# Selective-scan layer on one core: three small VectorE/GpSimd operations change engines, and one fetch moves up by a unit

## The chip, the cores and the metric

One core of a Trainium2 chip runs the whole program, four layers in one launch. The metric is the device time of one execution in microseconds, the median of several runs. VectorE is called DVE here, ScalarE ACT, GpSimd POOL, TensorE PE, and SP is the engine whose queue issues nearly all DMAs.

## The reference, cut to what matters

The input is eight images of 64 channels by 64 x 64. Layer 0 is a selective-scan block; layers 1 to 3 are attention and a small trained modifier, and the change doesn't touch them. In layer 0, after a norm, an input projection to a scanned half and a gate half z, and a depthwise convolution, four scans run over each image's 4096 places: along rows, along columns, and both backwards. Each has 128 channels and 16 states n:

```
h = h * exp(dt * A[n]) + dt * B[n] * u          # per place, channel and n
y = sum over n of h * C[n]                      # then summed over the four scans
y = layernorm(y) * silu(z);  out = x + y @ outproj
```

B and C come from projections of u and are the same for all 128 channels. silu(z) * layernorm(y) is the gating product that the change is about. dt is a softplus.

## The kernel before, in words

The scan layer is `scan_layer`. A *step* is one scan direction k and one chunk of 1024 places; an image has 16 steps, in the order k = 0, 2, 1, 3 (1, 3, 0, 2 for the last image), four chunks each. A step has 16 *units*, one for each state n; the code counts units as turns. The order of instructions on each engine is written out by hand, in the loop from L888 on.

In unit n of a step:

- SP loads C's row n, broadcast to 128 partitions, into a `ct` tile one unit ahead (L715; five `ct` buffers), and for the units 0, 3, 6 and 8 (`BY_POOL`, L704) B's row likewise into `bt`.
- ACT makes a = exp(dt * A[n]) two units ahead (L719).
- B * dt * u goes to a PSUM tile z in one of two ways. In `BY_POOL` units POOL multiplies `bt` by dt*u (L727) and ACT copies it to PSUM (L734). In the other twelve PE spreads B's row over the partitions (L737), and DVE multiplies that in place by dt*u (L764).
- DVE runs the scan h (L768), reading a from SBUF and z from PSUM. POOL multiplies h by C's row (L773), and PE adds the product into y's sum (L810, three units later), which frees the `ct` buffer.

For the spreading by PE, B is split into three bf16 pieces whose sum is B. This is done once for each chunk and each k of 0 and 1, so eight times an image, by `pieces`: fetch B (L673, SP), first piece (L677, ACT), subtract (L681, POOL), second piece (L684, ACT), third piece (L687, a subtraction on POOL), three stores (L692, SP), and a load in the spread form (L699, SP). These functions are called from `hooks`: a hook of unit n is called behind everything else of unit n. For a step with all seven pieces they stand at units 7 to 13. The softplus of the next step (`soft1`, `soft2` on ACT, `soft3` on POOL, L645) stands at 6, 7 and 8, and dt*u (L664, POOL) at 11.

Work of the neighbouring images (the norm, the convolution, the gate, the output projection) is a queue of small items (`Background`), at most one for each unit, and none at units 3, 6, 7 and 8 but for those without a PE part. The output part of the previous image, `norm_y` and `after`, is queued at unit 4 of step 0. Its `apply` puts y * rstd on DVE (L450) and gain and bias on ACT (L451), and behind these calls `multiply` (L564 to L566) for the block before: z *= y, 128 x 512, on POOL. PE projects the product out later (L573). z was fetched from DRAM three blocks ahead (L561).

Of the kernel before, what the change touches and what calls it, by code (L numbers as in the profile page):

```python
# [13 lines left out]
ALU = mybir.AluOpType  # L14
# [8 lines left out]
BK = 512  # L23
# [211 lines left out]
def scan_layer(cm, x_in, w, xh):  # L235

    tc, nc = cm.tc, cm.nc
    with ExitStack() as ctx:
# [63 lines left out]
        for e in range(2):  # L302
            r = slice(e * C, (e + 1) * C)
# [20 lines left out]
        def bank(name):  # L324
            return psum.tile([128, BK], F32, name=name, tag="mm")
# [226 lines left out]
        def after(b, y, zd, blocks=range(NBK)):  # L552

            xf = x_in[b].rearrange("c h w -> c (h w)")
            gated = {}

            def load(j):
                xr = work.tile([C, BK], F32, name="xr", tag="xr", bufs=3)
                nc.sync.dma_start(xr, xf[:, bass.ts(j, BK)])
                z = work.tile([DI, BK], F32, name="z", tag="z", bufs=3)  # L560
                nc.sync.dma_start(z, zd[:, bass.ts(j, BK)])  # L561
                gated[j] = (xr, z)

            def multiply(j):  # L564
                z = gated[j][1]
                nc.gpsimd.tensor_tensor(z, z, y[:, bass.ts(j, BK)], ALU.mult)  # L566

            def project_out(j):
                def make():
                    po = bank("ops")  # L570
                    xr, z = gated[j]
                    nc.tensor.matmul(po[:C], cm.ident[:C, :C], xr, start=True, stop=False)
                    nc.tensor.matmul(po[:C], wout, z, start=False, stop=True)  # L573
                    return po

                def use(po):
                    del gated[j]
                    xo = work.tile([128, BK], F32, name="xo", tag="sq")
                    nc.scalar.activation(xo[:C], po[:C], AF.Identity, bias=outb)
                    bg.later(lambda: nc.sync.dma_start(xh[b][:, bass.ts(j, BK)], xo[:C]))  # L580
                    if j + 3 in blocks:
                        load(j + 3)

                return make, use

            return norm_y(y, blocks, load, multiply, project_out)

        def ordered(t, k, c):
# [73 lines left out]
        def step_input(ctl):  # L662

            nc.gpsimd.tensor_tensor(ctl["dus"], ctl["dt"], ctl["ut"]["u"], ALU.mult)  # L664


        def pieces(ctl, low):

            by_place = "a n (j x) -> (n j) a x"

            def fetch():
                low["b"] = work.tile([128, 2, 128], F32, name="bw", tag="bw", bufs=1)
                nc.sync.dma_start(low["b"], low["bc"][:, :N].rearrange(by_place, x=128))  # L673

            def first():
                low["p"] = work.tile([128, 3, 2, 128], BF16, name="bp", tag="bp", bufs=1)
                nc.scalar.copy(low["p"][:, 0], low["b"])  # L677

            def subtract():
                low["r"] = work.tile([128, 2, 128], F32, name="br", tag="br", bufs=1)  # L680
                nc.gpsimd.tensor_tensor(low["r"], low["b"], low["p"][:, 0], ALU.subtract)  # L681

            def second():
                nc.scalar.copy(low["p"][:, 1], low["r"])  # L684

            def third():
                nc.gpsimd.tensor_tensor(low["p"][:, 2], low["r"], low["p"][:, 1], ALU.subtract)  # L687

            def store():
                low["bsd"] = dr.tile([2, 3 * N, CH], BF16, name="bsd", tag="bsd", bufs=8)  # L690
                for i in range(3):
                    nc.sync.dma_start(  # L692
                        low["bsd"][:, i * N : (i + 1) * N].rearrange(by_place, x=128),
                        low["p"][:, i],
                    )

            def get():
                ctl["bs"] = work.tile([3 * N, CH], BF16, name="bs", tag="bs")
                nc.sync.dma_start(ctl["bs"], low["bsd"][ctl["k"] // 2])  # L699

            return ([fetch, first, subtract, second, third, store] if ctl["k"] < 2 else []) + [get]


# [75 lines left out]
        def empty():  # L779

            if full:
                ctl = full.pop()
                nc.scalar.copy(
                    ordered(ctl["y"], ctl["k"], ctl["c"]),
                    ctl["ps"].rearrange("p (a b) -> p a b", b=S),
                )
# [85 lines left out]
        with tc.manual_schedule():  # L872
# [15 lines left out]
            for b in range(NB):  # L888
                for s in range(4 * NCH):


                    early, late = b == 0 and s + 1 < NCH, b == NB - 1 and s > 3 * NCH
                    if s + 1 < 4 * NCH:
                        nxt = prepare(b, s + 1)
                    else:
                        nxt = prepare(b + 1, 0)
                    bg.credit = 2 if b == NB - 2 else 1
                    idle = () if early or late else (3, 6, 7, 8)
                    hooks = {}
                    if nxt:  # L900
                        do = nxt["pieces"]
                        if early:
                            hooks = {
                                12: [do[0]], 13: [nxt["soft"][2], lambda: step_input(nxt)] + do[1:5],
                                14: do[5:6], 15: do[6:],
                            }
                        else:
                            hooks = {14 - len(do) + i: [f] for i, f in enumerate(do)}
                            for i, f in zip((6, 7, 8), nxt["soft"]):
                                hooks[i] = hooks.get(i, []) + [f]  # L910
                            hooks[11] = hooks.get(11, []) + [lambda: step_input(nxt)]

                    def ahead(do, m, *args):
                        if m < N:
                            do(ctl, m, *args)
                        elif nxt:
                            do(nxt, m - N, *args)

                    for n in range(N):
                        empty()  # L920
                        ahead(spread, n + 1)
                        slots = 0 if early or late else sum(m not in idle for m in range(n, N))
                        if n == LAG + 1:
                            bg.before(n in idle, slots)
                            begin_sum()
                        else:
                            if len(pending) > LAG:
                                sum_up()
                            if n == LAG + 5:
                                sum_up()  # L930
                            bg.before(n in idle, slots)
                        if (n + 5) % N in BY_POOL and not (early and n + 5 == N):
                            ahead(load, n + 5, 0)
                        ahead(load, n + 1, 1)
                        ahead(decay, n + 2)
                        save_state()
                        if n + 3 != N or not early:
                            ahead(product, n + 3)
                        unit(ctl, n)
                        bg.after()  # L940
                        for _ in range(bg.surplus(max(0, 11 - n)) if early else late):
                            bg.before()
                            bg.after()
                        for do in hooks.get(n, []):
                            do()
                        if n + 3 == N and early:
                            ahead(load, N, 0)
                            ahead(product, N)

                        if s == 0 and n == LAG + 2 and b > 0:  # L950
                            bg.add(after(b - 1, images[b - 1][2], images.pop(b - 1)[1]))
                        if late and n == LAG + 2:
                            c = 4 * NCH - s
                            bg.add(after(b, images[b][2], images[b][1], range(2 * c, 2 * c + 2)))
                        if s == (1 if b else NCH) and n == 0 and b + 1 < NB:
                            bg.add(later.pop(NCH, []))
                            start(b + 1)
                    if nxt:
                        if not nxt["first"]:
                            nxt["state"] = ctl["new"]  # L960
                    ctl = nxt
# [1154 lines left out]
```

## Time and profile before

| what | us |
|---|---|
| median of 3 runs | 12470.36 (12468.33 to 12488.72) |
| the profiled execution, its own time | 12474.25 |
| its span on the core | 12472.4 |
| scan layer within it | about 0 to 7200 |
| from 1000 to 6000: POOL busy in each 1000 | 957 to 965 |
| DVE | 937 to 948 |
| PE | 926 to 938 |
| ACT | 698 to 720 |
| DMA engines, mean share busy | 63 to 64% |

The rest of the page has three kinds of views. The shares and slices give each engine's busy time over the whole span and over 40 equal slices, as digits in tenths. The groups put together all instructions of one line, engine, operation and shape: count, then busy time in us and mean length of one in ns, then the idle time of the engine just before them and what ended it. The windows give the busy time of every engine in a chosen stretch, with the number of instructions, the granted PE clock as a share of full speed, the DMA share and the GB/s. The waits of 1000 to 7000 us are used too: SP waits 4277 us for PE's sums (L810) to free `ct` buffers, ACT waits 616 us for DVE's scans and 212 us for POOL's subtraction (L681), PE waits 326 us for DVE's scans, POOL waits 150 us for the load of `ct`, and DVE waits 144 us for PE's spread B.

### The profile page before, as it was taken

How to read it: one execution, taken by the hardware profiler on the slowest of the kernel's cores; microseconds unless marked ns; L12 is line 12 of the kernel's file. 1: busy time of each engine (PE TensorE's matmuls, PEld its weight loads, DVE VectorE, ACT ScalarE, POOL GpSimd, SP SyncE). 2: the span in 40 equal slices, each digit the busy share in tenths (PEclk: the TensorE clock that was granted, in tenths of full speed). 3: DMA queues.
4: the chain of work that ended last, by engine and by line, in shares of the span. 5: the costliest groups of instructions: out<-in, count | busy, mean ns of one | idle time of the engine just before them, and what ended most of it. 6: DMA issues, size and time to landing. Idle time of an engine off the chain costs nothing. (4 is left out here: it accounts for less than half of the span.)

```text
span 12472.4 us, 119759 instructions
## 1 busy us (share of the span) xinstructions
PE 11350.5 (91%) x38827; PEld 4100.1 (33%) x38827; DVE 10374.0 (83%) x7334; ACT 7820.0 (63%) x10296; POOL 7404.9 (59%) x3510
## 2 busy tenths in 40 slices
PE   7899998999999999999998889999987778999999
PEld 2233332332333323323322232332334463333333
DVE  4999999999999999999989857768687785676767
ACT  4776766766766767767666545546456584555554
POOL 4999999999999999999999800000005490000000
PEclk8999999999999999999989889999998789999999
DMA  3666656656666666666566510000011100000000
GB/s 110 208 210 211 210 200 221 211 202 214 210 203 212 207 212 213 202 218 205 198 206 204 179 34 18 12 25 6 18 38 40 41 24 23 17 6 17 6 11 6
DMA packets 541331, 1562.17 MB, mean 125 GB/s; under 512 B 127360, under 2 KB 144400, under 8 KB 538128
## 3 DMA queue, kind: packets, MB, share of 16 engines
q1 hardware_dynamic: 540688, 1554.36, 37.8%
q8 instruction: 310, 5.08, 0.2%
q14 instruction: 333, 2.73, 0.1%
HBM read 1456.41 MB, written 88.87 MB: 124 GB/s over the span
## 5 line engine op out<-in xcount | busy, mean ns | idle before, releaser
L773 POOL TENSOR_TENSOR ct<-ct,h 128x1024 f32<-128x1024 f32 x2048 | 4796.5, 2363 | 391.5 <-DMA ct<-bc 183.9
L768 DVE TENSOR_TENSOR_SCAN h<-a,state,z 128x1024 f32<-128x1024 f32 x1536 | 3572.4, 2342 | 96.0 <-ACT z L734 43.0
L1117 DVE TENSOR_TENSOR sum<-sum,ex 128x1024 f32<-128x1024 f32 x1920 | 2347.5, 1223 | 617.9 <-ACT ex L1110 483.0
L1110 ACT ACTIVATE ex<-sc 128x1024 f32<-128x1024 f32 x2048 | 1968.0, 1024 | 1359.7 <-PE sc L1105 1359.3
L810 PE MATMUL yps<-ct,ident 128*128 128x512 f32 x5632 | 2810.5, 629 | 6.9 <-POOL ct L773 6.8
L719 ACT ACTIVATE a<-dt,amat 128x1024 f32<-128x1024 f32 x2048 | 2345.0, 1146 | 718.1 <-DVE h L768 711.7
L764 DVE TENSOR_TENSOR z<-z,e 128x1024 f32<-128x1024 f32 x1536 | 1865.9, 1215 | 310.9 <-PE z L737 196.0
L1124 PE MATMUL av<-ex,v 128*64 128x512 f32 x8192 | 1950.0, 604 | 0.0
L1105 PE MATMUL sc<-q,k 16*128 16x512 f32 (+1 forms) x8192 | 1562.2, 623 | 4.2 <-ACT q L1098 3.1
L810 PEld LDWEIGHTS yps<-ct,ident 128*128 128x128 f32 x5632 | 1009.0, 194 | 1390.9 <-issue 1253.2
L737 PE MATMUL z<-bs,pick 48*128 48x512 bf16 x3072 | 957.0, 393 | 447.0 <-DVE h L768 398.5
L810 PE MATMUL yps<-ct,lno_cen 128*128 128x512 f32 x2560 | 1313.1, 646 | 0.5 <-POOL ct L773 0.5
L768 DVE TENSOR_TENSOR_SCAN h<-a,z 128x1024 f32<-128x1024 f32 x512 | 1163.1, 2283 | 80.8 <-ACT z L734 51.2
L727 POOL TENSOR_TENSOR bt<-bt,e 128x1024 f32<-128x1024 f32 x512 | 1210.8, 2365 | 4.5 <-DMA bt<-bc 4.5
L1431 POOL TENSOR_TENSOR gt<-gt,pad 128x1024 f32<-128x1024 f32 x16 | 34.9, 2184 | 1571.1 <-ACT gt L1430 1492.5
L1124 PEld LDWEIGHTS av<-ex,v 128*64 128x64 f32 x8192 | 512.2, 136 | 1332.8 <-issue 1278.9
L734 ACT COPY z<-bt 128x1024 f32<-128x1024 f32 x512 | 519.7, 1015 | 589.0 <-POOL bt L727 316.4
L1105 PEld LDWEIGHTS sc<-q,k 16*128 16x128 f32 (+1 forms) x8192 | 528.4, 184 | 1016.1 <-issue 977.2
L737 PEld LDWEIGHTS <-pick 48*128 48x128 bf16 x3072 | 177.7, 95 | 1709.6 <-DVE h L768 888.0
L810 PEld LDWEIGHTS yps<-ct,lno_cen 128*128 128x128 f32 x2560 | 468.6, 198 | 637.3 <-issue 560.7
L530 PE MATMUL vps<-pad,convd 128*128 128x512 f32 x1152 | 545.9, 597 | 0.0
L1804 DVE RECIPROCAL r<-e 128x512 f32<-128x512 f32 x128 | 420.6, 3322 | 0.0
(416 smaller groups left out, 10539.4 us busy)
## 6 DMA issues: line engine op xcount, KB each, us to landing
ct<-bc SPq DMA_DIRECT2D x2048, 512.0 KB
bt<-bc SPq DMA_DIRECT2D x512, 512.0 KB
x<-x SPq DMA_DIRECT2D x12, 2048.0 KB
bc<-e SPq DMA_DIRECT2D x128, 128.0 KB
zd<-z SPq DMA_DIRECT2D x64, 256.0 KB
z<-zd SPq DMA_DIRECT2D x64, 256.0 KB
x<-x SPq DMA_DIRECT2D x32, 512.0 KB
part<-x SPq DMA_DIRECT2D x128, 128.0 KB
```

Source lines behind the costliest of these rows:

```text
L530: nc.tensor.matmul(held[0].rearrange("p (r c) -> p r c", c=S), convd[:, t, :], pad[:, j * rows + dy : (j + 1) * rows + dy, dx : dx + S], s ...
L719: ctl["exp", n] = nc.scalar.activation(ctl["a", n], ctl["dt"], AF.Exp, scale=amat[:, ctl["k"], n : n + 1])
L727: nc.gpsimd.tensor_tensor(bt, bt, ctl["dus"], ALU.mult)
L737: nc.tensor.matmul(z[:, bass.ts(i, BK)], pick[:, n : n + 1].to_broadcast([3 * N, DI]), ctl["bs"][:, bass.ts(i, BK)], start=True, stop=True,)
L764: first = nc.vector.tensor_tensor(z, z, ctl["dus"], ALU.mult)
L768: nc.vector.tensor_tensor_scan(h[:, flip], a[:, flip], z[:, flip], 0.0 if state is None else state[:, n : n + 1], ALU.mult, ALU.add,)
L773: freed[at] = nc.gpsimd.tensor_tensor(ct, ct, h, ALU.mult)
L810: nc.tensor.matmul(ctl["ps"][:, bass.ts(i, BK)], ctl["mat"], ct[:, bass.ts(i, BK)], start=False, stop=(n == N - 1 and not ctl["turns"]),)
L1105: nc.tensor.matmul(sc[:, e, :], k[r : r + d, bass.ts(j, 128)], qs[i][r : r + d, :], start=True, stop=True,)
L1110: nc.scalar.activation(ex, sc, AF.Exp)
L1117: nc.vector.tensor_tensor(sums[i], sums[i], ex, ALU.add)
L1124: nc.tensor.matmul(avs[i][r, :], v[:, j, r], ex[:, e, :], start=(j == 0), stop=(j == TQ - 1))
```

## The change

Three instructions are issued on DVE instead of POOL: the gating product (64 in the program, 128 x 512 f32) and the two subtractions of `pieces` (64 each, 128 x 256; the second one's output is bf16). All their operands lie in SBUF. In the hooks of a step that isn't one of the first image's first four, the fetch of B moves from unit 7 to unit 6, and at units 6 to 8 the softplus comes ahead of the hook that was there, where before it came behind. Nothing else differs; on DVE's queue the product stands right behind L450 and the subtractions right behind the scans of units 9 and 11.

```diff
             def multiply(j):
                 z = gated[j][1]
-                nc.gpsimd.tensor_tensor(z, z, y[:, bass.ts(j, BK)], ALU.mult)
+                nc.vector.tensor_tensor(z, z, y[:, bass.ts(j, BK)], ALU.mult)
...
             def subtract():
                 low["r"] = work.tile([128, 2, 128], F32, name="br", tag="br", bufs=1)
-                nc.gpsimd.tensor_tensor(low["r"], low["b"], low["p"][:, 0], ALU.subtract)
+                nc.vector.tensor_tensor(low["r"], low["b"], low["p"][:, 0], ALU.subtract)
...
             def third():
-                nc.gpsimd.tensor_tensor(low["p"][:, 2], low["r"], low["p"][:, 1], ALU.subtract)
+                nc.vector.tensor_tensor(low["p"][:, 2], low["r"], low["p"][:, 1], ALU.subtract)
...
                             hooks = {14 - len(do) + i: [f] for i, f in enumerate(do)}
+                            hooks[6] = hooks.pop(7, [])
                             for i, f in zip((6, 7, 8), nxt["soft"]):
-                                hooks[i] = hooks.get(i, []) + [f]
+                                hooks[i] = [f] + hooks.get(i, [])
                             hooks[11] = hooks.get(11, []) + [lambda: step_input(nxt)]
```

## The prediction

> **What bounds the kernel now.** The span is 12472.4 us. The chain of work that ended last, the first view to try, reaches back only to about 9287 us, so it says nothing of the scan layer (about 0 to 7200 us), in which the whole change lies. I therefore read the engines' shares, and then windows.
>
> ```profile
> PE 11350.5 (91%) x38827; PEld 4100.1 (33%) x38827; DVE 10374.0 (83%) x7334; ACT 7820.0 (63%) x10296; POOL 7404.9 (59%) x3510
> ...
> DVE  4999999999999999999989857768687785676767
> ...
> POOL 4999999999999999999999800000005490000000
> ```
>
> POOL's 59% is an average: in slices 2 to 22, the scan layer, POOL and DVE are both full. The window of one step (16 units n of one chunk) says more. These are steps 0, 2, 3, 7, 8 and 9 of the fifth image; the second column is the step's length.
>
> ```profile
> core 0: us, PE busy (x) PEld busy (x) DVE busy (x) ACT busy (x) POOL busy (x), PEclk, DMA share, GB/s
> 3638.50:3691.90 53.40, 50.63 (x115) 15.31 (x114) 50.24 (x29) 37.88 (x60) 53.40 (x25) 0.97 0.60 205
> ...
> 3743.30:3804.00 60.70, 57.14 (x123) 17.77 (x124) 53.97 (x34) 37.56 (x57) 55.50 (x28) 0.92 0.67 226
> 3804.00:3861.10 57.10, 55.00 (x123) 17.07 (x124) 53.08 (x33) 36.58 (x55) 57.10 (x28) 0.97 0.66 211
> ...
> 4018.40:4075.70 57.30, 53.37 (x117) 18.98 (x118) 51.28 (x29) 46.91 (x63) 51.06 (x25) 0.91 0.62 206
> 4075.70:4128.40 52.70, 52.70 (x123) 18.24 (x122) 50.27 (x29) 44.26 (x60) 52.32 (x25) 1.00 0.67 220
> 4128.40:4181.80 53.40, 52.91 (x124) 18.38 (x123) 51.22 (x29) 44.96 (x60) 52.26 (x25) 1.00 0.66 222
> ```
>
> Steps 0 and 3 are POOL's (busy throughout), 8 and 9 PE's, and DVE is 0.4 to 4 us short of full in most: nothing moved onto DVE lies beside slack that is worth the name. A whole image takes 868 us, of which POOL is busy some 837 and DVE 820.
>
> The rows for the moved operations and for their nearest kin on DVE:
>
> ```profile
> L773 POOL TENSOR_TENSOR ct<-ct,h 128x1024 f32<-128x1024 f32 x2048 | 4796.5, 2363 | 391.5 <-DMA ct<-bc 183.9
> ...
> L566 POOL TENSOR_TENSOR z<-z,y 128x512 f32<-128x512 f32 x64 | 81.6, 1275 | 25.9 <-ACT y L451 25.9
> L687 POOL TENSOR_TENSOR bp<-br,bp 128x256 bf16<-128x256 f32 x64 | 43.4, 678 | 2.1 <-ACT bp L684 2.1
> L681 POOL TENSOR_TENSOR br<-bw,bp 128x256 f32<-128x256 f32 x64 | 43.2, 675 | 0.0
> ...
> L1399 DVE TENSOR_TENSOR max<-pad 128x512 f32<-128x512 f32 x4 | 2.8, 691 | 0.1
> ...
> L1401 DVE TENSOR_TENSOR pad<-max 128x256 f32<-128x256 f32 x4 | 1.7, 424 | 0.1
> ```
>
> **What the notes on the chip say, and the trace.** Every DVE operation of the scan's steps now reads at most one tensor from SBUF (the scan reads a from SBUF and z from PSUM, L764 e from SBUF and z from PSUM). The moved ones read two. The Trainium skill, "SBUF — State Buffer", section "Who interferes with whom", says that a DVE instruction with two SBUF inputs contends with a GpSimd instruction that reads SBUF: whichever starts first keeps the shared port for its whole instruction, and the other blocks. No row of this trace shows such a pair: L1399, L1401 and L1117 run while POOL is idle. The nearest is another form, a DVE TENSOR_SCALAR from SBUF to SBUF:
>
> ```profile
> 5.13 0.39 DVE L304 TENSOR_SCALAR ln_cen<-ident 64x64 f32<-64x64 f32 x2
> ...
> 7203.66 4.87 POOL L1339 MEMSET mv<- 128x1056 f32 x7
> ...
> 7205.11 1.08 DVE L117 TENSOR_SCALAR p_cen<-ident 64x64 f32<-64x64 f32 x1
> ...
> 7206.21 0.95 DVE L117 TENSOR_SCALAR p_cen<-ident 64x64 f32<-64x64 f32 x1
> ```
>
> The timeline (start, length) has the same 64x64 operation at about 0.19 us each with POOL idle, and at 1.08 and 0.95 us beside POOL's row of MEMSETs. Each of the two ended within 0.05 us of the end of one MEMSET (7206.14 and 7207.11): it lost the rest of the instruction that was under way, and no more. I go by the rule, with that manner of release.
>
> The same skill, "VectorE: DVE Perf Modes", section "Why `tensor_tensor` can't do 2×_2P or 4×", says that the second tensor takes the second port, so no faster mode is left; the trace agrees (424 ns for 256 elements, 691 for 512: about 1.04 ns an element). I use these rows.
>
> **The change, part by part.** (1) *Off POOL*: 64 products of 1.275 and 128 subtractions of 0.677 us, 81.6 + 86.6 = 168 us, per full image 8 x 1.275 + 16 x 0.677 = 21.0 us.
>
> (2) *Onto DVE*: 64 x 0.691 + 128 x 0.424 = 98.5 us of its own. To that comes the wait for the port. POOL's instruction under way is nearly always a 2.363 us product; half is 1.18 us. In the fifth image the ends of DVE's y operation, behind which the products go, lie 0.5 to 1.6 us (mean 1.2) ahead of the end of POOL's instruction. Bounds: 0 (no contention) and about 5 us (DVE gets in only when POOL runs out of ready work; a subtraction on POOL starts 5.0 to 6.2 us behind the scan of unit 9, which is POOL's backlog). I take 1.18: a product costs DVE 1.87 us, a subtraction 1.60, 40.6 us an image. POOL is blocked for the 0.4 to 0.7 us of each, some 12 us an image, still less than it is relieved of.
>
> (3) *What of this is on the path*, per image, by step:
> - 15, 0 and 1 (two subtractions each, 3.2 us): DVE idles 0.75, 3.2 and 0.4; POOL's relief can give back at most 1.35 of that, mostly in step 0. On the path 2.9, 2.2, 3.0.
> - 2 (four products, two subtractions, 10.7): its long waits are not POOL's (3.3 us for PE's rps behind the fetch of rstd, 2.1 for ACT's e) and stay. 10.0.
> - 3 (four products, 7.5): DVE waits 3.4 us there for POOL's ct; those go. 4.1.
> - 7 (3.2): DVE's idle lies in the step's first half, ahead of the hooks; in the second, 4047 to 4075.7, it is busy 28.41 of 28.70. 2.9.
> - 8, 9, 10 (3.2 each): PE is full, DVE idles 2.2 to 3.3, and PE's backlog covers that much. 3.2 in all.
>
> Together 28.3 us an image. Six images have all of it: 170. The first has only steps 7 to 10 and 15 (9 us; its early steps idle 20 to 28 us), the last all but step 15 (25); the last image's own eight products fall into steps where DVE idles 9 to 17 us: 0. Sum 204 us.
>
> (4) *ACT's waits* for POOL's subtraction (212 us in 1000 to 7000 us) nearly vanish, since DVE subtracts right behind scan 9 rather than 5 us later. That brings nothing: ACT is busy 37 of 53 us and afterwards waits for DVE's scans (616 us). The stores behind the third piece wait on SP today (103 us); the third piece ends at about scan 11's end + 1.6 instead of + 4.3 us, but scan 11 itself is later: 0.
>
> (5) *The fetch one unit earlier* (hook 7 to 6), and softplus ahead of the other hooks. It passes one ct load on SP's queue. In steps 15 to 2 B's store was issued 13 to 17 us ahead of the fetch, so nothing blocks; in steps 7 to 10 it is 7.15, and about 2 to 3.5 less after: the fetch may wait for the landing, with the ct load of unit 8 behind it. Bound: today's longest wait there is 1.7 us, 32 sets, 55 us; from below, POOL waits 184 us in all for ct. Gain: the first piece is ready 0.2 to 0.9 us ahead of scan 9's end, and DVE will now stand there; the earlier fetch keeps it so. I take 0. The SP queue gets no added DMA.
>
> 12474.25 (the profiled execution) + 204 = 12678; the median of the runs is 4 us lower, so **12675 us**, 1.6% slower.
>
> **Rivals.**
> (A) *No contention in this form.* Then DVE gains only 12.3 us an image and POOL loses 21. Steps 0, 1, 15 and 3 lose perhaps 0.5 to 1 us each, step 2 gains 3, since POOL's relief meets a DVE that is as full: about -1 us an image, 12465 us. For it: no two-input row shows a delay. Against: the rows above. It decides where the mean wait stays under about 0.2 us: from -7 us at no wait to 204 at 1.18 is some 180 us per us of wait, and 0.2% is 25 us. To be faster by more than that, steps 8 to 10 would have to shrink as well, which PE's full row forbids, unless DVE's lateness is what fills it.
> (B) *POOL wins each boundary* until it has nothing ready: 4 us a wait instead of 1.18, so 192 x 2.8 = 540 us more on DVE, most of it on the path, since POOL drains meanwhile: about 13150 us (12675 and nine tenths of it). For it: POOL's products follow one another without a gap. Against: DVE got in at the first boundary twice, at 7206.1 and 7207.1.
> (C) *The mechanism holds, but PE's and POOL's slack takes more of it*: half of the 204, about 12575.
>
> **How the numbers follow.** The forecast as worked 0.56, C 0.20, A 0.16 (within 0.2% 0.09, faster 0.07), B 0.08. The range, 12455 to 12840, takes in A as worked and a mean wait of up to about 2.1 us; it leaves out B, and A's part that is faster, some 0.15, and a few hundredths of the forecast's own tail. A measurement can tell about 0.2% from no change: faster 0.07, same 0.09, slower 0.84. The forecast's and C's own range is 12530 to 12840.
>
> **What would show it.** DVE's rows for L681 and L687 at about 1.6 us and for L566 at about 1.9, with minima near 0.42 and 0.69 and maxima near 2.8; L773's mean up by some 0.05 us, with maxima near 3.0. Under A all of these stay at 0.42, 0.69 and 2.46. Step 2 near 71 us and step 3 near 61; steps 8 to 10 within 2 us of now; ACT's wait for br gone; POOL's idle up to some 5%. I am wrong if these rows are long and the steps are not (C), or if DVE waits at L681 for ACT's first piece or at L566 for z's load.

## The result and the profile after

| | before | after |
|---|---|---|
| median of four runs, us | 12469.35 (12460.50 to 12488.72) | 12573.72 (12568.26 to 12586.33) |
| the profiled execution, its own time, us | 12474.25 | 12568.98 |
| its span, us | 12472.4 | 12567.2 |
| end of the scan layer (last scan of DVE), us | 7167.5 | 7269.3 |

The ratio is 1.0082, 95% interval 1.0066 to 1.0098: slower, by 104 us where the forecast had 204. The scan layer alone is 101.8 us longer, so all of it lies where it was looked for.

The shares of the whole span, and the slices, of the page after (the slices of DVE and POOL are those to compare with before):

```profile
PE 11406.5 (91%) x38827; PEld 4116.3 (33%) x38827; DVE 10595.9 (84%) x7526; ACT 7830.5 (62%) x10296; POOL 7281.6 (58%) x3318
...
DVE  5999999999999999999999858768687685666767
...
POOL 4998999999999998989989810000004490000000
```

DVE has gained 222 us of busy time and POOL lost 123 (neighbouring instructions overlap a little in the records, so sums of single rows come out somewhat larger), and in the scan layer POOL is now the one with 8s. PE's same 38827 matmuls take 56 us longer, at a mean granted clock of 0.941 where it was 0.946. The same steps of the fifth image as before (steps 0, 2, 3, 7, 8, 9; the second column is the length):

```profile
core 0: us, PE busy (x) PEld busy (x) DVE busy (x) ACT busy (x) POOL busy (x), PEclk, DMA share, GB/s
3674.50:3727.30 52.80, 50.75 (x114) 15.34 (x114) 51.55 (x32) 40.41 (x63) 51.20 (x22) 0.97 0.63 212
...
3784.10:3854.00 69.90, 61.73 (x124) 18.74 (x124) 64.24 (x41) 38.01 (x57) 52.20 (x22) 0.88 0.60 200
3854.00:3915.20 61.20, 56.91 (x120) 17.65 (x120) 58.44 (x37) 35.98 (x53) 52.47 (x22) 0.92 0.61 192
...
4070.60:4126.20 55.60, 51.71 (x120) 18.28 (x121) 52.61 (x32) 47.53 (x63) 51.69 (x23) 0.97 0.66 217
4126.20:4178.50 52.30, 52.30 (x122) 18.14 (x121) 51.42 (x32) 44.15 (x60) 51.24 (x22) 1.00 0.68 224
4178.50:4232.70 54.20, 53.71 (x125) 18.81 (x124) 52.94 (x31) 45.02 (x60) 51.54 (x23) 1.00 0.71 217
```

Steps 2 and 3 carry the cost; 0, 7, 8 and 9 are within 2 us of before, though DVE has two operations more in each. One image is one sample, so here is the mean over the images 2 to 6, worked out from the starts of DVE's scans in both traces, with DVE's idle time (the step's length less DVE's busy time):

| step | before | after | difference | forecast | DVE idle before | after |
|---|---|---|---|---|---|---|
| 2 | 60.8 | 66.4 | +5.6 | +10.0 | 6.8 | 2.6 |
| 3 | 57.0 | 62.2 | +5.1 | +4.1 | 4.0 | 1.9 |
| 15, 0, 1 together | 158.5 | 163.4 | +4.9 | +8.1 | 6.2 | 4.4 |
| 7 | 56.1 | 57.6 | +1.5 | +2.9 | 4.8 | 4.7 |
| 8, 9, 10 together | 161.3 | 160.8 | -0.5 | +3.2 | 8.5 | 3.6 |
| the image | 868.1 | 882.7 | +14.5 | +28.3 | 47.6 | 33.0 |

So DVE is busy some 29 us longer in an image; half of that came out of its own idle time, the other half made the image longer.

The moved operations in the scan layer (groups of 0 to 7300 us; busy, mean of one in ns, then the idle time ahead of them), and how single ones spread (one line's instructions: shortest, middle and longest in ns):

```profile
L566 DVE TENSOR_TENSOR z<-z,y 128x512 f32<-128x512 f32 x64 | 118.1, 1845 | 0.3 <-ACT y L451 0.3
L681 DVE TENSOR_TENSOR br<-bw,bp 128x256 f32<-128x256 f32 x64 | 103.9, 1624 | 39.4 <-ACT bp L677 39.4
L687 DVE TENSOR_TENSOR bp<-br,bp 128x256 bf16<-128x256 f32 x64 | 33.8, 528 | 1.9 <-ACT bp L684 1.9
```

```profile
L681 DVE TENSOR_TENSOR br<-bw,bp x64: 398/1404/5884, 78.6 to 6943.7; 128x256 f32<-128x256 f32 x64
L687 DVE TENSOR_TENSOR bp<-br,bp x64: 359/399/2378, 81.4 to 6951.0; 128x256 bf16<-128x256 f32 x64
L566 DVE TENSOR_TENSOR z<-z,y x64: 662/2251/2822, 1160.4 to 7293.6; 128x512 f32<-128x512 f32 x64
```

The shortest ones are each operation's own time (0.40, 0.36, 0.66 us), the rest is the wait for the port, which the trace counts as busy. In the mean the product and the first subtraction cost what the forecast said (1.87 and 1.60); the third piece hardly waits. The timeline (start, length) of step 7 of the same image shows why:

```profile
4099.88 4.69 POOL L773 TENSOR_TENSOR ct<-ct,h 128x1024 f32<-128x1024 f32 x2 [0.33 <-PE z L737]
...
4103.59 1.26 DVE L681 TENSOR_TENSOR br<-bw,bp 128x256 f32<-128x256 f32 x1
...
4104.54 2.53 POOL L645 TENSOR_TENSOR dt<-dt,e 128x1024 f32<-128x1024 f32 x1
...
4109.54 2.35 DVE L768 TENSOR_TENSOR_SCAN h<-a,state,z 128x1024 f32<-128x1024 f32 x1
...
4111.80 0.40 DVE L687 TENSOR_TENSOR bp<-br,bp 128x256 bf16<-128x256 f32 x1
...
4112.11 2.36 POOL L773 TENSOR_TENSOR ct<-ct,h 128x1024 f32<-128x1024 f32 x1 [0.42 <-DVE h L768]
```

At 4103.59 POOL is inside a product that ends at 4104.57; DVE is done 0.28 us behind that, and POOL's next instruction is 2.53 us long instead of some 2.36: now POOL was the blocked one. At 4111.80 POOL has nothing to do: its next product needs the very scan that the third piece follows, so the subtraction runs in its own 0.40 us. The wait at unit 9 has let POOL catch up for the wait at unit 11. The gating product has it the other way round. It stands behind the y operation of 0.66 us, which stands right behind a scan (step 3 of the same image), so POOL has just begun on that scan's h, and DVE loses nearly a whole instruction:

```profile
3828.30 0.66 DVE L450 TENSOR_TENSOR y<-y,rps 128x512 f32<-128x512 f32 x1
3828.62 2.36 POOL L773 TENSOR_TENSOR ct<-ct,h 128x1024 f32<-128x1024 f32 x1 [1.54 <-PE ops L572]
3828.88 2.64 DVE L566 TENSOR_TENSOR z<-z,y 128x512 f32<-128x512 f32 x1
```

In 4 of the 64 subtractions DVE let two boundaries pass and came in only at the third, as here in step 1 of the fifth image (POOL's first line is three products in a row, the last of which ends at 3757.73; two more instructions pass before DVE is done at 3762.61):

```profile
3750.73 7.00 POOL L773 TENSOR_TENSOR ct<-ct,h 128x1024 f32<-128x1024 f32 x3
...
3757.26 5.35 DVE L681 TENSOR_TENSOR br<-bw,bp 128x256 f32<-128x256 f32 x1
3757.67 2.37 POOL L645 TENSOR_TENSOR dt<-dt,e 128x1024 f32<-128x1024 f32 x1
3759.98 2.35 POOL L773 TENSOR_TENSOR ct<-ct,h 128x1024 f32<-128x1024 f32 x1
```

The waits of 1000 to 7000 us (sum, number, longest): ACT's for POOL's subtraction (212.0 before) is gone, ACT's for the scans is 297 us longer, and POOL, which had 45.1 us of waiting for scans, now has 200. DVE waits less for PE's spread B than before (143.7 us):

```profile
ACT a L719 <- DVE h L768: 913.2, 552, 4.3
...
POOL ct L773 <- DVE h L768: 200.2, 163, 4.5
...
DVE z L764 <- PE z L737: 109.6, 97, 4.1
```

So the slower PE didn't hold DVE up more than before, by these waits. Whether the lower granted clock took a part of the 104 us some other way isn't shown: among the runs of the kernel before alone, 0.001 of clock goes with 7 to 11 us of time, and they don't tell which follows which.

### The profile page after: what moved, and what is told of

Same layout as the page of the kernel before. It is cut to its first block, busy times and chain, and to the rows that moved or that the text cites. A ratio compares the mean times of both kernels' runs of the same rounds, so it can differ in the third digit from the quotient of the medians.

```text
span 12567.2 us, 119930 instructions
## 1 busy us (share of the span) xinstructions
PE 11406.5 (91%) x38827; PEld 4116.3 (33%) x38827; DVE 10595.9 (84%) x7526; ACT 7830.5 (62%) x10296; POOL 7281.6 (58%) x3318
## 5 line engine op out<-in xcount | busy, mean ns | idle before, releaser
L773 POOL TENSOR_TENSOR ct<-ct,h 128x1024 f32<-128x1024 f32 x2048 | 4812.8, 2367 | 613.3 <-DVE h L768 302.6
L810 PE MATMUL yps<-ct,ident 128*128 128x512 f32 x5632 | 2857.3, 638 | 0.2 <-POOL ct L773 0.2
L737 PE MATMUL z<-bs,pick 48*128 48x512 bf16 x3072 | 967.8, 397 | 519.6 <-DVE h L768 502.1
L737 PEld LDWEIGHTS <-pick 48*128 48x128 bf16 x3072 | 177.3, 95 | 1787.5 <-DVE h L768 1007.8
```

What stands on the lines that cost most here:

```text
L737: nc.tensor.matmul(z[:, bass.ts(i, BK)], pick[:, n : n + 1].to_broadcast([3 * N, DI]), ctl["bs"][:, bass.ts(i, BK)], start=True, stop=True,)
L773: freed[at] = nc.gpsimd.tensor_tensor(ct, ct, h, ALU.mult)
L810: nc.tensor.matmul(ctl["ps"][:, bass.ts(i, BK)], ctl["mat"], ct[:, bass.ts(i, BK)], start=False, stop=(n == N - 1 and not ctl["turns"]),)
```

## The experiments

All are timed against the kernel before on the same chip (its medians there lie between 12455 and 12470 us); "scan layer" is the end of DVE's last scan in the profile. The theory going in: the port costs DVE what the rows show, and the time is less than forecast because (a) POOL's relief pays for a part, or (b) DVE's lateness meets slack, or (c) part of the change gains.

**One part alone.** First only the product on VectorE, then only the subtractions with the new hooks (the product back on GpSimd).

```diff
 # e1, over before
-                nc.gpsimd.tensor_tensor(z, z, y[:, bass.ts(j, BK)], ALU.mult)
+                nc.vector.tensor_tensor(z, z, y[:, bass.ts(j, BK)], ALU.mult)
 # e2, over after
-                nc.vector.tensor_tensor(z, z, y[:, bass.ts(j, BK)], ALU.mult)
+                nc.gpsimd.tensor_tensor(z, z, y[:, bass.ts(j, BK)], ALU.mult)
```

> Only the gating products go to DVE; pieces and hooks as in the kernel before. Theory (port): a product on DVE waits for the rest of POOL's instruction under way, as in the changed kernel (mean 1.85 us, of which 0.67 its own); steps 2 and 3 carry most of the loss, so +60 to +90 us of the +104, DVE's row for L566 at 1.7 to 2.0 us. Rival (load alone): 64 products of 0.67 us are 43 us on DVE against 82 us less on POOL, so -20 to +20 us. Rival (the subtractions or the moved fetch cost the time): about 0.

> Only the two subtractions go to DVE, with the fetch moved; products on POOL. Port: 64 subtractions at about 1.6 us and 64 third pieces at about 0.5 us are 137 us of DVE, of which steps 7 to 10 hide nearly all, since PE is full there; +15 to +45 us. If the forecast's share on the path had been right, about +90 us. Load alone: 49 us of DVE against 87 us of POOL, -20 to 0 us.

Products alone: ratio 1.0047 (1.0034 to 1.0060), +63 us; steps 2 and 3 are 7.6 and 4.1 us longer, with the product's row first below. Subtractions alone: 1.0005 (0.9997 to 1.0013), +7 us, though DVE spends 147 us on them (second fence):

```profile
L566 DVE TENSOR_TENSOR z<-z,y 128x512 f32<-128x512 f32 x64 | 115.6, 1806 | 0.3 <-ACT y L451 0.3
```

```profile
L681 DVE TENSOR_TENSOR br<-bw,bp 128x256 f32<-128x256 f32 x64 | 111.0, 1734 | 39.5 <-ACT bp L677 39.5
...
L687 DVE TENSOR_TENSOR bp<-br,bp 128x256 bf16<-128x256 f32 x64 | 36.2, 565 | 1.9 <-ACT bp L684 1.9
```

So the products are slow as forecast, and the subtractions all but free. The two make 70 us together, not 104. The three intervals together leave some 27 us of that gap to chance, so whether a part of it is real is open. The scan layers of the profiles do add up (+72.9 and +23.5 against +101.8), but they don't decide it: the profiled executions of the two runs were 10 and 17 us above their own medians.

**The new hooks alone**: all three operations back on GpSimd.

```diff
 # e9, over before
+                            hooks[6] = hooks.pop(7, [])
...
-                                hooks[i] = hooks.get(i, []) + [f]
+                                hooks[i] = [f] + hooks.get(i, [])
```

> Only the order of the hooks: the fetch one unit earlier, softplus ahead; all three operations on POOL. Both theories: -10 to +10 us; a blocked ct load behind the earlier fetch would show as POOL waiting longer for ct and +20 to +55 us.

1.0001 (0.9993 to 1.0009). The fetch one unit earlier is worth nothing.

**The product without its wait.** Twice: put ahead of DVE's y operation, right behind the scan; and with its second input in PSUM.

```diff
 # e3, over after
-                    nc.vector.tensor_tensor(v, v, ps, ALU.mult)
-                    nc.scalar.activation(v, v, AF.Identity, bias=on_b, scale=on_g)
                     if j - 1 in blocks:
                         multiply(j - 1)
+                    nc.vector.tensor_tensor(v, v, ps, ALU.mult)
+                    nc.scalar.activation(v, v, AF.Identity, bias=on_b, scale=on_g)
 # e6, over after
-                nc.vector.tensor_tensor(z, z, y[:, bass.ts(j, BK)], ALU.mult)
+                other = y[:, bass.ts(j, BK)] if ps is None else ps
+                nc.vector.tensor_tensor(z, z, other, ALU.mult)
```

> The changed kernel with the product ahead of the y operation on DVE's queue, so right behind a scan: the same instructions, another phase to POOL. Port: POOL, drained, starts its product on the same scan's end 0.3 us later than DVE can, so DVE gets the port first: L566's mean falls from 1.85 to 0.7 to 1.0 us, and the time by 30 to 60 us, to +45 to +75 us over before. Load alone, or a slower DVE: L566 and the time don't move (+104).

> The changed kernel, but seven of an image's eight products read rstd's row from PSUM as second operand instead of y from SBUF (so the multiplication by y is left out): one SBUF input, the same place and length. Port: those products take 0.66 us whatever POOL does, and the time falls by 30 to 60 us, to +45 to +75 us. Rival (DVE is slowed by something else at that place, its waits on ACT or POOL's writes): they stay at 1.5 to 2.5 us and the time at about +104.

```profile
L566 DVE TENSOR_TENSOR z<-z,y 128x512 f32<-128x512 f32 x64 | 75.2, 1175 | 4.4 <-ACT y L453 4.4
```

```profile
L567 DVE TENSOR_TENSOR z<-z,rps 128x512 f32<-128x512 f32 x53 | 36.1, 680 | 0.0
```

Moved 0.66 us ahead, the product is 0.67 us shorter in the mean (first row; 1.175 us, not the 0.7 to 1.0 expected) and the kernel loses 46 us less against before than after does: 12522.55 us, 1.0051 (1.0039 to 1.0063), +58. With one input in PSUM (second row; 53 of the 64 products multiply by rstd's row instead of y, so the output is another) it takes 0.68 us at POOL's full load and never waits. The scan layer of that kernel ends at 7189.1, 80 us ahead of after, for 74 us less of DVE (118.1 less 36.1 and the 8.4 of the other eleven products). Its whole time, 29221 us, isn't used: with the other values the later layers issue more matmuls (65969 in all instead of 38827). The wait is two SBUF inputs' and the products' wait is nearly all on the path.

**Where the subtraction stands.** Unit 10 instead of 9, with the product first (e7) and with the product on GpSimd (e10); and only the third piece on VectorE (e4).

```diff
 # e7 over e3, e10 over e2
+                            hooks[10] = hooks.pop(9, []) + hooks.get(10, [])
 # e4, over before
-                nc.gpsimd.tensor_tensor(low["p"][:, 2], low["r"], low["p"][:, 1], ALU.subtract)
+                nc.vector.tensor_tensor(low["p"][:, 2], low["r"], low["p"][:, 1], ALU.subtract)
```

> The changed kernel with both phases mended: the product ahead of the y operation, and the first subtraction behind the scan of unit 10 instead of 9 (with the second piece behind it on ACT). In the changed kernel POOL still has a backlog at the end of scan 9 (the subtraction then waits 1.2 us) but none at the end of scan 11 (the third piece waits nothing); at scan 10 the backlog is about 0.9 us. Port: L681's mean falls from 1.6 to 0.5 to 1.0 us; if subtractions are hidden anyway, the time stays at the +58 us of the run with the product ahead alone, within 20; if their wait is on the path, it falls to about +15 us.

> Products on POOL, both subtractions on DVE with the first at unit 10. Beside the run with subtractions at 9 and 11 (+7 us). Port: DVE's cost falls by some 60 us; -25 to +5 us over before. If subtractions are hidden anyway: +0 to +10 us.

> The kernel before with the third piece alone on DVE. The first subtraction stays on POOL, so POOL starts the third's scan with its backlog larger than in the changed kernel. Port by phase: POOL's backlog at scan 11 decides; where it still runs, the third waits up to 2.4 us, and L687's mean is 1 to 2 us; where it is drained, 0.4. The time: -15 to +25 us. Load alone: 26 us on DVE against 43 off POOL, 0 to -15 us.

Misses, all three: e7 1.0096 (1.0081 to 1.0110), +117 us; e10 1.0050 (1.0037 to 1.0063), +63; e4 1.0055 (1.0039 to 1.0071), +75, for one small subtraction. First e10's row, then e4's:

```profile
L681 DVE TENSOR_TENSOR br<-bw,bp 128x256 f32<-128x256 f32 x64 | 146.6, 2290 | 38.6 <-ACT bp L677 38.6
```

```profile
L687 DVE TENSOR_TENSOR bp<-br,bp 128x256 bf16<-128x256 f32 x64 | 169.1, 2642 | 64.1 <-ACT bp L684 63.7
```

I had thought unit 11 a good place and unit 10 half as good. But without a wait ahead of it POOL has its backlog there too: alone, the third piece takes 2.64 us on average (second row), with 12 of 64 over 5 us. It was short in after because the first subtraction had drained POOL.

**Is there slack where PE is full?** The subtractions on VectorE only in steps 7 to 10 (e8), only in steps 15, 0, 1 and 2 (e8b).

```diff
 # e8, over e9, for both subtractions; e8b with 0 for 1
-                nc.gpsimd.tensor_tensor(low["r"], low["b"], low["p"][:, 0], ALU.subtract)
+                eng = nc.vector if ctl["k"] == 1 else nc.gpsimd
+                eng.tensor_tensor(low["r"], low["b"], low["p"][:, 0], ALU.subtract)
```

> Products on POOL, hooks moved, subtractions on DVE only for k = 1, whose pieces fall into steps 7 to 10 of an image, where PE is full; for k = 0 on POOL. If PE's full steps hide DVE's work: -15 to +5 us. If POOL's relief is what hides it, the same size of result in both halves.

> The other half: subtractions on DVE only for k = 0, in steps 15, 0, 1 and 2, where PE isn't full. If PE hides the other half, this half carries all the loss of the two: +10 to +35 us. The forecast had 8.1 us an image for steps 15, 0 and 1, so some 60 us.

1.0009 (1.0002 to 1.0015), +10 us, and 0.9998 (0.9988 to 1.0007), -6 us. That PE's backlog alone hides them falls: they cost no more in steps 15 to 2.

**What is POOL's relief worth?** GpSimd does the subtractions too, into an unused tile (e11, over e2); neither engine does them (e12: second and third pieces are zeros by ScalarE, so B is rounded to bf16; products on GpSimd); GpSimd does a product of the same size (y times y, unused) beside VectorE's (e14b, over e1); B in two pieces (e13, third one left out; e15, second one written by GpSimd directly, both with some 16 bits of B). The declarations of unused tiles are left out here and in e17 below.

```diff
 # e11, over e2 (and the same behind the other subtraction)
                 nc.vector.tensor_tensor(low["r"], low["b"], low["p"][:, 0], ALU.subtract)
+                nc.gpsimd.tensor_tensor(low["j"], low["b"], low["p"][:, 0], ALU.subtract)
 # e12, over e9 (and the same for the third piece)
-                nc.gpsimd.tensor_tensor(low["r"], low["b"], low["p"][:, 0], ALU.subtract)
-                nc.scalar.copy(low["p"][:, 1], low["r"])
+                nc.scalar.activation(low["p"][:, 1], low["b"], AF.Identity, scale=0.0)
 # e14b, over e1
                 nc.vector.tensor_tensor(z, z, y[:, bass.ts(j, BK)], ALU.mult)
+                nc.gpsimd.tensor_tensor(junk, y[:, bass.ts(j, BK)], y[:, bass.ts(j, BK)], ALU.mult)
 # e13, over before (and 2 for 3 in the store and the load)
-                nc.gpsimd.tensor_tensor(low["p"][:, 2], low["r"], low["p"][:, 1], ALU.subtract)
 # e15, over e13
-                nc.gpsimd.tensor_tensor(low["r"], low["b"], low["p"][:, 0], ALU.subtract)
-                nc.scalar.copy(low["p"][:, 1], low["r"])
+                nc.gpsimd.tensor_tensor(low["p"][:, 1], low["b"], low["p"][:, 0], ALU.subtract)
```

> Both subtractions on DVE for all sets (products on POOL, as in the run of +7 us), and POOL does them as well, into a tile that nobody reads: DVE's load and waits stay, POOL's relief of 87 us is taken back. If the relief is what paid for DVE's 147 us: +60 to +120 us. If DVE's time was hidden behind PE: within 15 us of the +7.

> The second and third piece of B are zeros made by ACT, so B is rounded to bf16 and both subtractions are left out on both engines; products on POOL. What POOL's relief of 87 us is worth with nothing in return: -50 to -90 us if POOL sets the pace in the steps with pieces; -10 to -30 us if DVE is as full there.

> The kernel before with the product on VectorE, and POOL given one more product of the same size (y times y, into a tile that nothing reads) right where its own stood; so VectorE pays as in the run with the product alone on VectorE (+63 us), but POOL is relieved of nothing. If POOL's relief pays for the products at the rate of the subtractions (about 0.8 us of time for 1 us of POOL), 82 us of POOL cost some 65 us more: +130 us against the kernel before. By the forecast's valuing (3.4 us an image, in step 3 alone) it is +85 to +90 us. If the relief in the steps 2 and 3 is worth nothing, +63 us. The product's wait should stay near 1.8 us in all cases, L566 at 110 to 130 us in all.

> The kernel before with B carried in two bf16 pieces, not three: the third piece, its subtraction on POOL (43 us), its store and its third of the spread loads are left out, and nothing moves to VectorE. B then has some 16 bits instead of 24. If a microsecond of POOL is worth 0.8 us in the scan layer, as leaving out both subtractions gave (-69 us for 87), this gives about -35 us: faster than both kernels. If POOL's relief is worth only the forecast's 1.35 us an image in the steps 15, 0 and 1, about -5 us, no change that can be measured. SP's queue gets shorter by 64 stores; SP waits mostly for PE's sums, so that is expected to bring nothing of itself.

> B in two bf16 pieces as in the run before (GpSimd relieved of one subtraction, 43 us), but here GpSimd writes the second piece itself and ScalarE makes none, so ScalarE waits for nothing there. If GpSimd's relief counts, and nothing else, it is like the run with two pieces where ScalarE still waited: -7 us, no change that can be measured. If ScalarE's wait counts, -50 to -70 us, faster than both kernels. If only the two together count, between these.

e11: 1.0064 (1.0051 to 1.0076), +80 us, against e2's +7; e12: 0.9946 (0.9933 to 0.9959), -69 us. These two looked like a proof that GpSimd's 87 us are worth some 70. They aren't. e14b: 1.0052 (1.0037 to 1.0068), +68, against +63 without the ballast: 69 us of GpSimd cost 5, though VectorE's products also became 17 us shorter beside the ballast (first row below, against 115.6), so up to some 22. In the profiles the forecast's one gain shows: DVE's idle time of 4.0 us in step 3 falls to 0.5 in e1 and only to 3.3 in e14b. e13: 0.9992 (0.9983 to 1.0000), -7; e15: 0.9990 (0.9984 to 0.9997), -16, for 43 us each. And e11's own rows (the last two) show another cost:

```profile
L566 DVE TENSOR_TENSOR z<-z,y 128x512 f32<-128x512 f32 x64 | 98.8, 1543 | 0.0
```

```profile
L681 DVE TENSOR_TENSOR br<-bw,bp 128x256 f32<-128x256 f32 x64 | 140.3, 2192 | 38.9 <-ACT bp L677 38.9
...
L689 DVE TENSOR_TENSOR bp<-br,bp 128x256 bf16<-128x256 f32 x64 | 54.6, 853 | 1.9 <-ACT bp L686 1.9
```

The ballast makes VectorE's subtractions 48 us longer in all (195 instead of 147 us), so of e11's 73 us over e2 some 25 would be left for the 87 us of GpSimd, if each us of that waiting costs a us.

**What else did leaving both out change?** ScalarE's wait for the subtraction (e16: second piece zeros by ScalarE, both subtractions kept, so B has some 16 bits), and the data: two of three pieces that TensorE multiplies are zeros (e17: zeros in both, both subtractions kept, into tiles that nothing later reads, so B is rounded to bf16; e12b: e12 again beside it).

```diff
 # e16 and e17, over before
-                nc.scalar.copy(low["p"][:, 1], low["r"])
+                nc.scalar.activation(low["p"][:, 1], low["b"], AF.Identity, scale=0.0)
 # e17 besides
-                nc.gpsimd.tensor_tensor(low["p"][:, 2], low["r"], low["p"][:, 1], ALU.subtract)
+                nc.gpsimd.tensor_tensor(low["j"], low["r"], low["p"][:, 1], ALU.subtract)
+                nc.scalar.activation(low["p"][:, 2], low["b"], AF.Identity, scale=0.0)
```

> The kernel before, but ScalarE makes the second piece as zeros from B, so it doesn't wait for GpSimd's first subtraction (212 us of waiting in the scan layer); GpSimd does both subtractions as before (B is then carried in the first and the third piece, some 16 bits). The forecast held that this wait costs nothing: no change, 0 plus or minus 15 us. If this wait, and not GpSimd's time, is what leaving out both subtractions saved, -50 to -70 us.

> The second and third pieces are zeros made by ScalarE, as in the run that left both subtractions out (B is then rounded to bf16), but GpSimd still does both subtractions, into tiles that nothing later reads: GpSimd's load is that of the kernel before, and only the data that TensorE multiplies differ, two of three pieces being zeros. If GpSimd's relief was the 69 us, this is like the kernel before (0 plus or minus 15 us). If the zeros were it, by way of TensorE's granted clock, -50 to -70 us, with a mean clock of some 0.949 against 0.946.

> The run that left both subtractions out, again, on the same chip as the run before it: -60 to -75 us. Both theories expect this; it is here so that the two are compared directly.

e16: 0.9997 (0.9989 to 1.0006). The wait is worth nothing. e17: 0.9976 (0.9966 to 0.9986), -28 us, with every instruction's load as before but for one small one more of ScalarE for each set; e12b: 0.9948 (0.9934 to 0.9962), -63. So the zeros give 28 us, and leaving out GpSimd's 87 us gives the other 35: 0.4 us for one, not 0.8. How zeros give it is open. The mean clock granted to TensorE was 0.9477 in the nine runs of e17 and 0.9462 in the 13 of before beside them; among those 13, 0.001 of clock goes with some 9 us of time, so the clock could account for about 13 of the 28 us, if time follows clock, which no run shows.

**Step by step.** What remains is slack. I matched each step that has subtractions in the second to seventh image (48 steps) with the same step of before, and sorted them by what DVE spent there on them:

| run | steps | DVE's subtractions, us a step | step longer by, us |
|---|---|---|---|
| e2 | 42 | 1.67 | 0.18 |
| e2 | 6 | 6.06 | 3.58 |
| e10 | 41 | 2.59 | 1.49 |
| e10 | 7 | 5.05 | 3.55 |
| e11 (GpSimd not relieved) | 37 | 2.19 | 0.91 |
| e11 | 11 | 6.66 | 5.33 |
| e4 | 37 | 1.82 | 0.57 |
| e4 | 11 | 6.44 | 2.84 |

The first row of each run has the steps under 3 us, the second those above 4. Where the addition is under 3 us, 1.1 to 1.5 us a step disappear, with POOL relieved or not; of the long ones 44 to 80% is on the path. Most of what e2 loses in these steps (21.5 of 29 us) comes from the six with a long wait. Where they disappear shows in DVE's waits: for PE's spread B it waits 114.9 us in e2 (1000 to 7000 us; sum, number, longest) where it was 143.7.

```profile
DVE z L764 <- PE z L737: 114.9, 91, 4.2
```

The reading is that DVE, held up by the port, comes later to data that PE has ready by then; no run changes PE alone to test it. (This leans on one profile each, and e2's is the execution 17 us above its median; single steps of two traces also differ by a us or two for reasons of their own, but the 48 steps without subtractions differ by -0.4 to +0.2 on average in these runs.)

## Why the prediction was wrong

**Right: the mechanism and the size of two of its three waits.** Two SBUF inputs on DVE wait for POOL's instruction (L566 1.845 us for 1.87, L681 1.624 for 1.60, minima at the operations' own time, product maxima at 2.82 for 2.8), and one input in PSUM makes the wait vanish (e6). The wait of two SBUF inputs is what the Trainium skill, "SBUF — State Buffer", section "Who interferes with whom", states; the traces here agree, and show that DVE mostly gets in at the next end of a POOL instruction. For L681 the close number is in part luck: 60 of the 64 take 1.35 us in the mean, and four long ones of 5.4 to 5.9 us lift it. Rival A is out. Rival B is out as the rule, but happens now and then: 4 of 64 in after, 7 in e2, 12 in e11 and in e4.

**Right: the products' share.** With the measured product, the forecast's sum has 7.4 us in step 2, whose waits stay, and 4.0 in step 3, where POOL's relief gives 3.4 back. In e1 the steps grew by 7.6 and 4.1, and the idle times moved that way (7.0 us left in step 2, 0.5 in step 3). In after, with the subtractions beside them, it was 5.6 and 5.1.

**Failed: "(2) a subtraction 1.60 us", for the third piece.** It took 0.53, so DVE's moved operations took 256 us (118.1 + 103.9 + 33.8) instead of 325. I took half of POOL's instruction for every subtraction's wait, as if the moments were random. They aren't: an operation behind a scan has a fixed place in POOL's cycle, and the wait at unit 9 sets the cycle for unit 11. Put the measured costs into the forecast's own sum and leave all else as it was, and the 204 us become about 140. This term is some 64 of the 100 us that the forecast was off.

**Failed: part (3), what DVE's idle time takes.** The same sum gives the subtractions alone some 60 us; e2 measured +7 (-4 to +16). Outside steps 8 to 10 the forecast held DVE's idle time nearly fixed wherever the wait wasn't POOL's: "its long waits are not POOL's ... and stay" for step 2, and "nothing moved onto DVE lies beside slack that is worth the name". But DVE idled 47.6 us in an image, mostly in waits for others, and such waits shrank when DVE came later. Step 2's idle time fell from 6.8 us to 4.0 in e2 and 2.6 in after, and the image's to 38.2 and 33.0 (means over the images 2 to 6 of one profile each). All in all idle time gave 14.6 us an image in after, with 29 put on DVE, where the forecast let it give 12.3 (40.6 less 28.3) of 40.6. The forecast also read one image: its step 15 idles 0.75 us, the mean of five is 2.75.

So the time is rival C's, 12575, and slack did take more than I gave it. But C left the third piece at 1.60 and put the whole difference on slack, where that wait was nearly two thirds of it; that its number came out is in part luck.

**Smaller terms.** ACT's 212 us of waiting is worth nothing (e16, 0.9997), and so is the earlier fetch (e9, 1.0001), as forecast. That POOL would be blocked some 12 us an image was far too much: L773's mean went from 2.363 to 2.367 us and L645's from 2.357 to 2.429, some 16 us in the whole program. POOL's relief, which the forecast let count for little, is worth little: 0.1 to 0.4 us a us in e13, e14b, e15, and e12b against e17. Its other effect, shorter waits of DVE (e11), I hadn't thought of.

**No better kernel.** No version with the whole computation was faster than before by 0.2%; e15 (two pieces) at -0.1% gives up bits of B. Of the change, the subtractions in steps 15 to 2 alone are free (e8b), the products cost wherever DVE has two SBUF inputs.

## To carry to other kernels

An elementwise operation with two SBUF inputs, moved to VectorE beside a busy GpSimd, costs its own time and the rest of GpSimd's instruction under way; work the wait out from where the operation stands in GpSimd's cycle, not as half an instruction, and put it where GpSimd waits for VectorE itself, or give it a PSUM input. An engine's idle time beside an added operation isn't fixed because another engine ends it: DVE's waits for PE shrank when DVE came later. Read it over several repeats of the step, not one: 1.1 to 1.5 us a step were absorbed here, of waits of 5 us and more mostly half or less, so ask for the longest waits before the mean. An experiment that replaces work by zeros also changes the data, and needs its own control: here the zeros were 28 of 63 us. An unused operation added as ballast isn't neutral either: it made VectorE's waits 17 us shorter in one run here and 48 us longer in another.

## What the runs showed of the hardware

- A DVE operation that loses the port is shown as busy for the whole wait: 0.40 us of work as 1.4 in the middle case, up to 5.9. Busy time of DVE is thus no measure of its work here.
- POOL's instruction that starts behind it can be longer too: 2.53 us instead of 2.36 behind a subtraction of 256 elements (this one is softplus's product, L645: 2.43 us in the mean instead of 2.36).
- Sometimes DVE lets two ends of POOL's instructions pass (4 to 12 of 64). What decides this wasn't found (counted are those over 5 us in after, e2, e11 and e4).
- Zeros in two thirds of the bf16 operand of L737's matmuls made the kernel 28 us faster (e17), the other instructions the same in number and shape but for one small one more of ScalarE for each set of pieces.
